# Selective scan on one core: the projection of u for both halves of the tokens side by side in two column tiles of TensorE

## Chip, cores, metric

One core of a Trainium2 chip runs the whole program: a two-layer network in one launch, all in float32. The metric is the time of one execution on the device, in microseconds (us). Engines are named as the profile names them: PE is TensorE (its weight loads are listed apart as PEld), DVE is VectorE, ACT is ScalarE, POOL is GpSimd, SP is SyncE, which issues the DMAs.

## The reference

Layer 0 is an attention over 4096 tokens of 4 images and a recurrent network over the same tokens; layer 1 is a selective scan and a mixture of experts. The change concerns the selective scan alone. With D = 256 channels, N = 16 states, R = 8 ranks, K = 4 directions and L = 4096 tokens of each of 4 images, it computes:

```
x_dbl = einsum('bkdl,kcd->bkcl', xs, x_proj_w)       # xs: u in 4 directions, c = R + 2N rows
dts_r, Bs, Cs = x_dbl[:, :, :R], x_dbl[:, :, R:R+N], x_dbl[:, :, R+N:]
dt = softplus(einsum('bkrl,kdr->bkdl', dts_r, dt_proj_w) + dt_proj_b)
h  = h * exp(dt * A) + (dt * u) * B                  # over the tokens, for each of D x N states
y  = sum over n of h * C
```

followed by sums over the directions, a norm, a gate and an output projection.

## The kernel before

`model` runs the stages one after the other: `attention`, `rnn`, `selective_scan`, `experts`. Inside the selective scan the function `scans` does the recurrence. A *window* is W = 500 tokens, that is NB = 4 blocks of T = 125, of one direction k; there are 33 windows in each of 4 directions, in the order k = 2, 3, 0, 1, so 132 windows. In k = 2 and 3 the tokens run backwards. A window has 16 *tiles*: 4 blocks times 4 quarters of the 16 states. A tile holds 4 states of all 256 channels (two halves h of 128 partitions) for 125 tokens, and one instruction of DVE, `tensor_tensor_scan` (L1315), runs its recurrence over 1016 columns.

Per tile: PE fills one of the two buffers `db` in PSUM with dt * u * B, by 16 small matmuls on 32 rows each (`fill`, L1291: for h = 0 on the rows of the block's number, for h = 1 two row groups further), and in the meantime adds zeros to the sum `y` (L1300). ACT computes the decays exp(dt * A) (L1256) into a ring ahead of time. DVE scans. ACT carries the last state of a block over to the next block's tile (`carry`, L1336). POOL multiplies the states by C (`times_c`, L1349), for which a DMA spreads the C rows over all partitions (`load`, L1268). Every second tile, PE sums the products over the states into `y` (`sum_of`, L1366: 8 matmuls in four 64x64 tiles). At a window's end ACT copies `y` out (`finish`, L1387); in all directions but k = 3 something that was there before is added to `y` first (`add_other`, L1377).

What the tiles of a window need is made ahead by the generator `project` (L1134 to L1241). It begins 40 turns before the window's first tile, is cut into steps by `yield turn`, and a loop over turns p runs each step when its turn comes. The order of all work is written out by hand: in each turn `finished`, `fill` of the next tile, `carry`, `scan`, `sums`, `times_c`, the load of C five turns ahead, `before`, `decay`, and then the steps of `project` that are due, first those of the window that began earlier. The steps, with their turns before the change:

- at -40 u is loaded; at -33 and -31 two matmuls (L1144) project its two halves of channels onto 128 rows x 500 tokens in `mm[:, 0]`: the dt ranks at rows 0 to 7 and again at 96 to 103, B at 32 to 47, C at 64 to 79;
- at -30 ACT adds a one and writes this to `xd` (L1149), and a DMA writes the C rows to `c_rows` in DRAM (L1151); at -29 ACT copies the B rows, in four overlapping quarters of a block, to `b_rows` (L1158);
- at -23 two matmuls of 9 rows (L1163) give dt for the two halves of channels in the two banks of `mm`, from rows 0 and 96 (so in two row tiles);
- at -22 to -20 ACT computes the softplus (L1182, L1185, L1187, L1188, L1190); at -19 and -18 DVE takes a maximum of two forms of it (L1195); at -17 POOL multiplies by u (L1198);
- at -15 the B rows are transposed (L1203) into `mm[:, 1]`; at -14 and -13 ACT copies them and dt * u (L1206, L1227), and DVE and POOL spread B onto diagonals (L1213, L1221);
- at -12 two DMAs write `b_other` (L1232), at -11 PE transposes dt * u (L1239), at -10 ACT copies it (L1241).

Since windows are 16 tiles apart, the step at -31 of one window falls in the turn of the step at -15 of the window before, and -33 in that of -17. The two PSUM banks `mm` are one tile that all these steps share, of which there is one.

```
        for h, turn in enumerate((-33, -31)):
            yield turn
            nc.tensor.matmul(
                x_ps[:, :W], w_x[:, h, k, :], v.u[:, h, :], start=h == 0, stop=h == ND - 1
            )
```

In the trace a float32 matmul has two records, one for each of its passes. The tiles of the first window take the turns 0, 2, 4, 5, 6 and so on; from then on each turn has one scan.

## Time and profile before

| what | value |
|---|---|
| time, median of 3 runs | 9429.01 us (9418.11 to 9439.51) |
| the profiled execution: its time | 9417.97 us |
| its span, first to last instruction | 9416.2 us |
| mean granted TensorE clock | 0.971 |
| first scan begins, last scan ends | 3582.7 us, 8748.5 us |
| scans (L1315) | 2112 of 2256 ns, 4671.3 us busy |
| products with C (L1349) | 2112 of 2152 ns, 4459.8 us busy |
| decays (L1256) | 4224 of 715 ns, 3018.2 us busy |
| projection of u (L1144) | 528 records, median 687 ns |
| dt (L1163) | 528 records, median 580 ns |
| xd (L1149), b_rows (L1158) | 132 each; 677 ns, 630 ns |
| softplus: L1182, L1185, L1187, L1188, L1190 | 132 each; 995, 991, 1133, 999, 1018 ns |
| dt maximum on DVE (L1195) | 264 of 654 ns |

The distance from one window's first scan to the next is 39.27 us in the directions 2, 0 and 1, and 38.43 us in direction 3; the first window takes 46.11 us. In the profile's groups, "idle before, releaser" tells how long an engine stood still just ahead of an instruction and what let it go on. Busy shares on the page are means over all stages; the fullest engine of the page need not be the one that sets the end of a stage.

### The profile page before, as it was taken

What the parts mean: (1) busy time and instruction counts of PE and PEld (TensorE: products, weight loads), DVE (VectorE), ACT (ScalarE), POOL (GpSimd) and SP (SyncE); (2) the same over time, 40 slices, a digit from 0 to 9 for tenths busy, and PEclk for the clock granted to TensorE, in tenths of its full rate; (3) what the DMA queues carried; (4) which work ended last, traced back from release to release, by engine and by line L of the source; (5) the groups of instructions that cost most, each with busy time, mean ns of one, the idle gap of its engine ahead of it and who ended that gap; (6) DMA issues with size and microseconds to landing.
All of it is one profiled execution on the core that took longest, in us unless ns stands there. A gap on an engine that the chain in (4) does not pass through costs nothing. (4 is left out here: it accounts for less than half of the span.)

```text
span 9416.2 us, 237919 instructions
## 1 busy us (share of the span) xinstructions
PE 8705.1 (92%) x102194; PEld 4318.3 (46%) x102194; DVE 8349.7 (89%) x5102; ACT 7121.8 (76%) x10926; POOL 4993.6 (53%) x2433
## 2 busy tenths in 40 slices
PE   7999999999988888999999999999999999999766
PEld 3333333333323334555555555555555555555223
DVE  6999999999978318999999999999999999999764
ACT  3888888888856467888888888888888888888321
POOL 0000000000001017999999999999999999999100
PEclk8999999999999898999999999999999999999887
DMA  4000000000011335666666656666666666666634
GB/s 169 36 8 35 8 10 35 8 8 8 10 52 56 115 135 151 173 173 173 172 171 167 165 164 162 161 171 173 173 173 173 173 173 173 173 173 168 231 111 184
DMA packets 530963, 1164.77 MB, mean 124 GB/s; under 512 B 76818, under 2 KB 444506, under 8 KB 502106
## 3 DMA queue, kind: packets, MB, share of 16 engines
q1 hardware_dynamic: 529882, 1149.30, 42.0%
q8 instruction: 807, 13.22, 0.6%
q14 instruction: 274, 2.24, 0.1%
HBM read 828.51 MB, written 182.15 MB: 107 GB/s over the span
## 5 line engine op out<-in xcount | busy, mean ns | idle before, releaser
L1315 DVE TENSOR_TENSOR_SCAN states<-decays,db 128x1016 f32<-128x1016 f32 x2112 | 4671.3, 2256 | 109.1 <-ACT decays L1336 60.5
L1349 POOL TENSOR_TENSOR products<-states,c_ring 128x1000 f32<-128x1000 f32 x2112 | 4459.8, 2152 | 294.8 <-DVE states L1315 173.4
L1256 ACT ACTIVATE decays<-dt,a_logs 128x500 f32<-128x500 f32 x4224 | 3018.2, 715 | 86.6 <-DVE states L1315 0.5
L1291 PEld LDWEIGHTS db<-b_diag,dtu_t 32*128 32x128 f32 x16896 | 2051.1, 187 | 1523.1 <-DVE states L1315 927.4
L1291 PE MATMUL db<-b_diag,dtu_t 32*128 32x128 f32 x16896 | 2429.4, 283 | 245.1 <-DVE states L1315 226.2
L1291 PE MATMUL db<-b_other,dtu_t 32*128 32x128 f32 x16896 | 2454.2, 284 | 0.0
L1300 PE MATMUL y<-zeros 32*128 32x128 f32 x14720 | 2122.0, 283 | 0.0
L1291 PEld LDWEIGHTS db<-b_other,dtu_t 32*128 32x128 f32 x16896 | 2048.0, 186 | 0.3 <-issue 0.2
L1366 PE MATMUL y<-products,ident 64*64 64x500 f32 x16896 | 2018.8, 592 | 1.1 <-POOL products L1349 1.1
L1300 PEld LDWEIGHTS y<-zeros 32*128 32x128 f32 x14720 | 1771.9, 186 | 0.0
L342 DVE TENSOR_TENSOR total<-total,ring 128x2048 f32<-128x2048 f32 x768 | 1706.9, 2285 | 32.3 <-ACT ring L304 31.6
masks.py:197 POOL MEMSET ident<- 128x128 f32 x6 | 1.2, 206 | 2915.6 <-SPq L181 2622.9
L304 ACT ACTIVATE ring<-sa 128x2048 f32<-128x2048 f32 (+3 forms) x667 | 1153.7, 1738 | 273.8 <-PE sa L289 262.2
L314 PE MATMUL av<-ring,v_at 128*32 128x256 f32 (+1 forms) x16128 | 1096.1, 389 | 6.2 <-ACT o L323 5.7
L1366 PEld LDWEIGHTS y<-products,ident 64*64 64x64 f32 x16896 | 541.2, 132 | 696.7 <-issue 568.1
L314 PEld LDWEIGHTS av<-ring,v_at 128*32 128x32 f32 x16128 | 421.4, 109 | 950.9 <-issue 748.9
L304 ACT ACTIVATE ring<-sb 128x1536 f32<-128x1536 f32 (+2 forms) x585 | 800.6, 1375 | 73.6 <-PE sb L289 63.8
L289 PE MATMUL sa<-q_at,k_at 32*128 32x512 f32 x4898 | 701.4, 640 | 20.6 <-issue 14.3
L289 PE MATMUL sb<-q_at,k_at 32*128 32x512 f32 x3294 | 624.0, 641 | 0.0
L1336 ACT COPY decays<-states 128x8 f32<-128x8 f32 x2048 | 405.3, 198 | 212.2 <-DVE states L1315 196.0
L289 PEld LDWEIGHTS sa<-q_at,k_at 32*128 32x128 f32 x4898 | 192.4, 183 | 354.6 <-issue 177.1
L339 DVE TENSOR_TENSOR total<-ring 128x2048 f32<-128x2048 f32 x128 | 288.6, 2287 | 67.0 <-ACT ring L304 66.6
(217 smaller groups left out, 8023.7 us busy)
## 6 DMA issues: line engine op xcount, KB each, us to landing
c_ring<-c_rows SPq DMA_DIRECT2D x2112, 250.0 KB, 4.8
b_other<-b_diag SPq DMA_DIRECT2D x264, 512.0 KB, 6.2
weights<-in_w SPq DMA_DIRECT2D x32, 1024.0 KB, 13.0
u<-u_r SPq DMA_DIRECT2D x60, 500.0 KB, 6.4
y_r<-sum SPq DMA_DIRECT2D x60, 500.0 KB, 4.7
u<-u_c SPq DMA_DIRECT2D x60, 500.0 KB, 6.4
y_c<-sum SPq DMA_DIRECT2D x60, 500.0 KB, 5.1
x<-x SPq DMA_DIRECT2D x96, 256.0 KB, 2.6
```

The costliest lines, as they stand in the source:

```text
L289: nc.tensor.matmul(s[:, m, :], k[rows, tokens(t)], q[rows, chunk(chunk_state["c"])], start=True, stop=True,)
L304: nc.scalar.activation(ring[:, lo : lo + n, :], s[:, at : at + n, :], AF.Exp)
L314: nc.tensor.matmul(chunk_state["av"][rows, some], chunk_state["v"][:, t, rows], ring[:, at + i, some], start=t == 0, stop=t == NJ - 1 and ...
L339: nc.vector.tensor_add(total, sums[g - 2], w)
L342: nc.vector.tensor_add(sums[g % 2], sums[g % 2], w)
L1256: nc.scalar.activation(to, dt, AF.Exp, scale=scale)
L1291: nc.tensor.matmul(bank.rearrange("p (n t) -> p n t", n=4)[:, :, to : to + 32], v.dtu[rows, h, s, :], b[rows, s, 4 * self.q : 4 * self.q + ...
L1300: nc.tensor.matmul(y[:, idle // 2, :P], zeros[rows], zeros[rows], start=False, stop=False)
L1315: nc.vector.tensor_tensor_scan(order(self.slot(states)), order(self.slot(decays, shift)), order(self.db[:, SKIP + shift :][:, : 2 * LANE]) ...
L1336: nc.scalar.copy(self.edge(later.slot(decays), later.v.into), last)
L1349: nc.gpsimd.tensor_mul(to, h, c)
L1366: nc.tensor.matmul(to, ident[rows, rows], of, start=begins, stop=ends)
```

## The change

The projection puts two halves of the window's tokens (blocks 0 and 1, blocks 2 and 3) beside each other: 64 rows each, in two column tiles of PE, where dt is at rows 0 to 7, B at 32 to 47 and C at 48 to 63 of each half. All four matmuls of 250 columns are issued at turn -33. `xd` has half as many columns and comes at -31, the B rows at -30, in two copies; the C rows go out in two DMAs. dt comes from rows 0 and 64, where the two halves of the tokens lie: four matmuls of 9 rows by 250 columns, bank j of `mm` for the half j of the tokens, and in each bank the two halves of the channels behind each other. So `mm` is read and written in another order afterwards, by a view of four runs of 250 columns; `e`, `bound` and `dt` keep their layout and are only viewed in the same way.

```diff
-DT_ROWS = 0, 96
+DT_ROWS = 0, 64
...
-    w_dt = cst.tile([P, K, P], F32, name="w_dt")
+    w_dt = cst.tile([P, K, ND, P], F32, name="w_dt")
...
-    for h, row in enumerate(DT_ROWS):
-        nc.sync.dma_start(w_dt[row : row + R + 1], a["w_dt"][:, :, h * P : (h + 1) * P])
+    for row in DT_ROWS:
+        nc.sync.dma_start(
+            w_dt[row : row + R + 1], a["w_dt"].rearrange("r k (h d) -> r k h d", h=ND)
+        )
...
+    def in_halves(of):
+        return of.rearrange("p h (j t) -> p h j t", j=2)
...
-        x_ps = mm[:, 0]
-        for h, turn in enumerate((-33, -31)):
-            yield turn
-            nc.tensor.matmul(
-                x_ps[:, :W], w_x[:, h, k, :], v.u[:, h, :], start=h == 0, stop=h == ND - 1
+        yield -33
+        x_ps = mm[:, 0, :WH]
+        for h in range(ND):
+            for j in range(2):
+                nc.tensor.matmul(
+                    x_ps[HALF * j : HALF * j + HALF],
+                    w_x[:, h, k, :],
+                    v.u[:, h, j * WH : (j + 1) * WH],
+                    start=h == 0,
+                    stop=h == ND - 1,
+                )
+        yield -31
+        xd = work.tile([P, WH], F32, tag="xd", name="xd", bufs=1)
+        nc.scalar.activation(xd, x_ps, AF.Identity, bias=one)
+        v.c_rows = dram.tile([NB, N, T], F32, tag="c", name="c_rows")
+        for j in range(2):
+            nc.sync.dma_start(
+                v.c_rows[2 * j : 2 * j + 2].rearrange("i n t -> n i t"),
+                xd[HALF * j + 48 : HALF * j + 48 + N].rearrange("n (i t) -> n i t", t=T),
             )
         yield -30
-        xd = work.tile([P, W], F32, tag="xd", name="xd", bufs=1)
-        nc.scalar.activation(xd, x_ps[:, :W], AF.Identity, bias=one)
-        v.c_rows = dram.tile([NB, N, T], F32, tag="c", name="c_rows")
-        nc.sync.dma_start(
-            v.c_rows.rearrange("i n t -> n i t"),
-            xd[64 : 64 + N].rearrange("n (i t) -> n i t", i=NB),
-        )
-        yield -29
         b_rows = work.tile([32 + N, NS, NB, 32], F32, tag="b_rows", name="b_rows", bufs=1)
-        for to, of in quartered(xd[32 : 32 + N], b_rows[32:], False):
-            nc.scalar.copy(to, of)
+        for j in range(2):
+            of = xd[HALF * j + 32 : HALF * j + 32 + N]
+            nc.scalar.copy(
+                b_rows[32:, :, 2 * j : 2 * j + 2],
+                bass.AP(of.tensor, of.offset, [of.ap[0], [STEP, NS], [T, 2], [1, 32]]),
+            )
         yield -23
-        pts = mm[:, :, :W]
-        for h, row in enumerate(DT_ROWS):
-            rows = slice(row, row + R + 1)
-            nc.tensor.matmul(pts[:, h], w_dt[rows, k, :], xd[rows], start=True, stop=True)
+        pts = mm[:, :, :W].rearrange("p j (h t) -> p h j t", h=ND)
+        for h in range(ND):
+            for j, row in enumerate(DT_ROWS):
+                rows = slice(row, row + R + 1)
+                nc.tensor.matmul(pts[:, h, j], w_dt[rows, k, h, :], xd[rows], start=True, stop=True)
...
-        bound = low[:, : ND * W].rearrange("p (h t) -> p h t", h=ND)
+        bound = in_halves(low[:, : ND * W].rearrange("p (h t) -> p h t", h=ND))
+        e = in_halves(e)
...
+        dt = in_halves(v.dt)
...
-            nc.vector.tensor_max(v.dt[:, h], pts[:, h], bound[:, h])
+            nc.vector.tensor_max(dt[:, h], pts[:, h], bound[:, h])
```

The weights are laid out to match: `w_x` has 64 rows a direction instead of 128, and each of the two row tiles holds the dt weights of all 256 channels.

More of the change, by code (lines that the diff above doesn't have):

```diff
@@ L1019, in scans @@
     TILES = Q * NB
-    HALF = P // 2
+    HALF, WH = P // 2, W // 2
     S = T + 2
@@ L1809, in apart @@
     def apart(w):
-        out = np.zeros((K, P, D), w.dtype)
-        out[:, 32 : 32 + N], out[:, 64 : 64 + N] = w[:, R : R + N], w[:, R + N :]
-        for row in DT_ROWS:
-            out[:, row : row + R] = w[:, :R]
+        out = np.zeros((K, P // 2, D), w.dtype)
+        out[:, :R] = w[:, :R]
+        out[:, 32 : 32 + N], out[:, 48 : 48 + N] = w[:, R : R + N], w[:, R + N :]
         return out
@@ L1840, in laid_out @@
         "b_conv": i["L1_conv_conv_b"].reshape(ND, P).T,
-        "w_x": apart(i["L1_conv_x_proj_w"]).reshape(K, P, ND, P).transpose(3, 2, 0, 1),
+        "w_x": apart(i["L1_conv_x_proj_w"]).reshape(K, P // 2, ND, P).transpose(3, 2, 0, 1),
         "w_dt": np.concatenate(
```

## The prediction

> **What bounds the kernel now.** I read the page first, then who waits on VectorE (DVE), then the timelines of one window of the scans (the one from 4375.07 to 4414.34 us), engine by engine. The page's first part names TensorE as the fullest engine:

> ```profile
> PE 8705.1 (92%) x102194; PEld 4318.3 (46%) x102194; DVE 8349.7 (89%) x5102; ACT 7121.8 (76%) x10926; POOL 4993.6 (53%) x2433
> ```

> That is an average over four layers. In the scans (first scan 3582.7, last 8748.5 us: 5165.8 us, 132 windows of 16 scans) all four engines are near full: in that one window of 39.27 us PE is busy 37.54, DVE 38.15, POOL 37.02 and ACT 33.16 us, at a granted clock of 1.00. So the question is which wait ends last. The waits of DVE over the stage:

> ```profile
> DVE states L1315 <- ACT decays L1336: 60.5, 99, 1.0
> DVE states L1315 <- PE db L1291: 28.5, 102, 2.2
> DVE dt L1195 <- ACT low L1190: 27.6, 125, 0.2
> ```

> All gaps of DVE in the stage add up to 137 us: no change of this stage that leaves DVE's own work alone can win more. The timeline of DVE in the chosen window shows where they sit:

> ```profile
> 4390.10 4.43 DVE L1315 TENSOR_TENSOR_SCAN states<-decays,db 128x1016 f32<-128x1016 f32 x2
> 4395.15 4.47 DVE L1315 TENSOR_TENSOR_SCAN states<-decays,db 128x1016 f32<-128x1016 f32 x2 [0.61 <-ACT decays L1336]
> 4399.79 4.43 DVE L1315 TENSOR_TENSOR_SCAN states<-decays,db 128x1016 f32<-128x1016 f32 x2 [0.17 <-PE db L1291]
> 4404.44 0.68 DVE L1195 TENSOR_TENSOR dt<-mm,low 128x500 f32<-128x500 f32 x1 [0.22 <-ACT low L1190]
> ```

> Numbering a window's scans 0 to 15, these waits stand before scans 8 and 10 and before the first dt maximum; 0.11 us stands before scan 6. The ACT timeline (idle time and its releaser in brackets):

> ```profile
> 4393.96 0.99 ACT L1387 COPY sum<-y 128x1000 f32<-128x1000 f32 x1 [1.62 <-PE y L1366]
> ...
> 4403.39 1.02 ACT L1190 ACTIVATE low<-low 128x1000 f32<-128x1000 f32 x1
> ...
> 4415.48 0.17 ACT L1206 COPY b_sb<-mm 128x16 f32<-128x16 f32 x1 [0.73 <-PE mm L1144]
> 4415.54 0.63 ACT L1227 COPY quarters<-dtu 128x512 f32<-128x512 f32 x1
> 4417.88 0.68 ACT L1149 ACTIVATE xd<-mm,one 128x500 f32<-128x500 f32 x1 [1.70 <-DVE b_diag L1213]
> ```

> From 4393.96 to 4404.41 ACT never stops, and the dt maximum starts when it gets through. It starts when PE's sums (L1366) end at 4393.90. The PE timeline, of the fills only the records after an idle stretch:

> ```profile
> 4380.81 0.37 PE L1291 MATMUL db<-b_diag,dtu_t 32*128 32x128 f32 x1 [0.60 <-DVE states L1315]
> ...
> 4408.45 1.11 PE L1144 MATMUL mm<-u,w_x 128*128 128x500 f32 x2
> 4410.10 0.37 PE L1291 MATMUL db<-b_diag,dtu_t 32*128 32x128 f32 x1 [0.54 <-DVE states L1315]
> ...
> 4414.33 1.10 PE L1144 MATMUL mm<-u,w_x 128*128 128x500 f32 x2
> ```

> From 4380.81 to 4393.90 PE has no gap either, and at 4380.81 it had waited for scan 1, which ended at 4380.75. So the window is one loop: PE from scan 1's end to the sums (13.09 us, with 0.06 before), ACT to the dt maximum (10.48), DVE without a gap from 4404.44 to the next window's scan 1 (4420.02, 15.58): 13.15 + 10.54 + 15.58 = 39.27 us, the measured period. Only what lies on this loop moves the time. In the 33 windows of k = 3 (38.43 us) nothing is added from another scan, PE's piece is about 0.84 us shorter, and the rest is the same.

> **The change, part by part.**

> *Projection of u, before.* Two matmuls of 500 columns, 1.11 us at 4408.45 (between the fills of scans 14 and 15) and 1.10 us at 4414.33 (between those of scans 0 and 1). Neither lies on the loop: behind the first PE idles 0.54 us, and behind the second it runs without a gap to about 4419.4 and idles 0.60 us before it may fill scan 3. The second is removed. That moves the fills of scans 1 and 2 about 1.0 us forward; scan 1 starts 1.2 us after its fill ends anyway, and the idle time before the fill of scan 3 grows from 0.60 to some 1.6 us. Value 0. What is late next is unchanged: that fill, which waits for scan 1.

> *Projection of u, after.* Four matmuls, 128 rows by 64 columns, 250 streamed columns each, all at the first place. Nearest row: four column tiles of full height in the attention,

> ```profile
> 2000.25 1.07 PE L314 MATMUL av<-ring,v_at 128*32 128x256 f32 x16
> ```

> Sixteen records of 256 columns in 1.07 us: the records start in fours, 7 ns apart, and the fours 0.216 to 0.24 us apart. So four steps (two passes of two accumulations), with side by side tiles for free. The new block also has four steps, of 250 columns: 1.05 us, against 1.11 now. The margin is 0.54 us: PE's next fill must start at 4410.10, and from there fill, sums and fill run without a gap to 4414.19, where the next scan 0 waits for nothing but has nothing to spare (it starts 0.15 us after the fill; before scan 6, which does wait, this distance is 0.14). So a block above about 1.7 us is paid in full in each window.

> [...] The row: in L314 the loads of the second pass (110 ns) start 2 ns after the first pass and the next pass follows at 0.216 us, on the same 128 rows. I take the row: 1.05 us, no cost.

> *dt from two row tiles.* Before, two matmuls of 9 rows by 500 columns on rows 0 and 96; after, four of 250 on rows 0 and 64. Per row tile two passes of 500 or four of 250: the same stream. What changes is who shares the row tiles with the fills on either side. In the windows that run backwards (k = 2, 3) these use rows 0 and 64, so dt starts after the fill and not beside it: up to 0.1 us later for the fill behind. Forwards (k = 0, 1) they use 32 and 96, so dt can lie beside them, up to 0.8 us of PE gained. Both act on the wait before scan 10 (0.17 us) and no further, because the dt maximum behind it waits for ACT in any case: what scan 10 gains or loses, up to 0.22 us, that wait gives back. Value 0.

> *ACT.* xd halves: 0.677 us for 500 columns becomes about 0.677 - 250 x 0.00084 = 0.47 (the slope from L1256 with 500 to L1187 with 1000 elements, and from 256 to 512 in the copies L1227, is 0.84 to 0.88 ns). b_rows becomes two copies of 256 elements, 0.41 each (row L1227) for 0.63. Sum 1.29 against 1.31 us. xd comes one turn sooner, ahead of the b_diag product on DVE, and no longer waits 1.70 us for it; b_sb loses its 0.73 us wait for L1144. All of it is ACT time between 4414.6 and 4420, and ACT idles 1.62 us later, at the sums, waiting for PE. What queues behind xd is the carry of scan 15, needed by scan 1 some 2.5 us later, and behind b_rows the carry of scan 0, ready about 4417.2 and needed at 4420.5 by scan 2. Value 0.

> *ACT on the loop.* L1182, L1185 and L1188 now walk mm in four runs of 250 instead of two of 500, and these do lie on the loop. Bound from below 0. From above: the copies of 8 and 16 runs (0.411 and 0.635 us for 256 and 512 elements) leave 198 and 208 ns beside the elements, so at most 1.3 ns a run, under 10 ns for the three. The two dt maxima on DVE likewise: runs of 32 in L1213 cost as much per element (1.09 ns) as the runs of 500 in L1195. I take 0; at the upper end 132 x 0.01 = 1.3 us.

> *DMA.* c_rows goes out as two writes instead of one: 0.32 us more on SP, and it is moved past one c_ring load. Now SP stands at this write until 4418.58, waiting for xd, with two c_ring loads queued behind; with xd sooner these leave some 3 us sooner. POOL waits 22.3 us for c_ring in the whole stage and is not on the loop. Value 0. The weights of the projection are half as large, those of dt twice: loaded once, behind VectorE's initial memsets.

> *Start of the scans.* Before the first scan there is no cover, and matmuls take twice as long there. In the second window's projection PE runs from 3559.21 to 3563.71; b_sb, the quarters and everything to the first scan follow it. After: four steps of about 0.45 us and the 0.6 us of B transposes, ready about 3561.8. The first scan comes about 2 us sooner. This is the one gain that I count.

> *Sum.* 132 x 0 - 2 us: span 9416.2 becomes 9414, and 9418.0 for the profiled run becomes 9416. The profiled run lies 11.0 us below the median of the three runs (9429.0), so on the median's scale: 9427.

> **The rivals.** No change: the loop of PE, ACT and DVE stays as it is. For it: its pieces add up to the period. 9427, with the spread of the three runs (-10.9, +10.4) about 9412 to 9444. A measurement of this kernel tells 0.2% (19 us) from no change.

> Slower, by the column tiles: the block at 4408.45 takes more than 1.7 us, and the fills of scans 15 and 0 slip. [...] Against it: L314 and the free start of its loads. [...]

> Slower, by the access patterns: three activations and two maxima on the loop have more runs; from 0.14 us a window on it shows. The copies speak against it. At 0.2 us a window: 9453.

> Faster: PE's relief shortens the loop after all, because the wait before scan 10 goes (0.17 x 99 + 0.09 x 33 = 20 us) and ACT is ready sooner than I think. Against it: ACT has no gap from 4393.96 on. 9407.

> **How the numbers follow.** No change 0.77, column tiles 0.09, patterns 0.06, faster 0.08. The range takes in nearly all of the first case and the near ends of the others: 9405 to 9448. Faster by over 0.2%: 0.08; slower: 0.15; within: 0.77.

> **What would show it.** Right: window periods of 39.27 and 38.43 us as before; one block of projection of some 1.05 us with PE idle about 0.6 us behind it; over 1.4 us idle before the fill of scan 3; no wait of xd for b_diag; the waits before scan 8 and the dt maximum still there; the wait before scan 10 smaller in k = 0, 1 alone and that before the maximum larger by as much. Wrong: a wait before scan 0 (column tiles), longer L1182, L1185 or L1188 (patterns), or a shorter stretch of ACT between sums and maximum.

## The result, and the profile after

The changed kernel takes 9579.67 us (median of 4 runs, 9575.05 to 9583.58), the kernel before beside it 9432.17 us: a ratio of 1.0158 [1.014, 1.0176]. The forecast was 9427 us, no change. The profiled execution has a span of 9581.7 us instead of 9416.2, and a mean granted clock of 0.95 instead of 0.971. The page's first part and the clock's row, after:

```profile
PE 8697.4 (91%) x103250; PEld 4349.3 (45%) x103250; DVE 8340.0 (87%) x5102; ACT 7126.9 (74%) x11058; POOL 4999.6 (52%) x2433
...
PEclk8999999999999978999999999999999999999887
```

Nothing here stands out: each engine works as long as before, in a longer span. The loss is in the scans: first scan to last takes 5313.5 us instead of 5165.7, which is 147.8 of the 165.5 us (13 lie ahead of the first scan and vary by as much between runs, 5 behind the last). The sums by stretch for 3600 to 8700 us, first after, then before; the third number from the end is the clock:

```profile
3600.00:8700.00 5100.00, 4711.70 (x67088) 2816.52 (x67088) 4823.12 (x2539) 4211.49 (x8119) 4690.07 (x2282) 0.96 0.60 166
```

```profile
3600.00:8700.00 5100.00, 4863.22 (x68001) 2868.17 (x67996) 4970.52 (x2612) 4317.95 (x8206) 4816.49 (x2347) 1.00 0.63 170
```

The clock of 0.96 instead of 1.00 is the figure to follow. DVE's waits in the scans after:

```profile
DVE states L1333 <- ACT decays L1274: 100.5, 99, 2.3
DVE states L1333 <- ACT decays L1354: 61.0, 101, 1.0
DVE states L1333 <- PE db L1309: 51.3, 89, 3.1
DVE dt L1213 <- ACT low L1207: 41.7, 115, 0.5
DVE states L1333 <- PE y L1318: 34.2, 55, 0.6
```

The second and the fourth of these were there before. The first and the last are new: 99 waits of 1 us, nearly all before scan 4, and 55 of 0.6 us before scan 6. (In 43 more windows the wait before scan 6 is put down to the fill, L1309, and is in the third line.) In DVE's timeline of one window (its first scan starts at 4416.54 us) they are the waits at 4428.03 and 4433.08:

```profile
4418.73 1.20 DVE L1231 TENSOR_TENSOR b_diag<-mm,ident 128x1024 f32<-128x1024 f32 x1
...
4422.60 4.42 DVE L1333 TENSOR_TENSOR_SCAN states<-decays,db 128x1016 f32<-128x1016 f32 x2
4428.03 4.43 DVE L1333 TENSOR_TENSOR_SCAN states<-decays,db 128x1016 f32<-128x1016 f32 x2 [1.01 <-ACT decays L1274]
4433.08 4.43 DVE L1333 TENSOR_TENSOR_SCAN states<-decays,db 128x1016 f32<-128x1016 f32 x2 [0.62 <-PE db L1309]
4438.13 4.47 DVE L1333 TENSOR_TENSOR_SCAN states<-decays,db 128x1016 f32<-128x1016 f32 x2 [0.62 <-ACT decays L1354]
```

The wait at 4428.03 is put down to ACT, but the fill of that scan (L1309) ends on PE at 4427.89: PE was late. PE's timeline of the same window, the projection, the sums and the pause:

```profile
4410.65 1.06 PE L1150 MATMUL mm<-u,w_x 128*64 128x250 f32 x8
...
4417.72 1.91 PE L1384 MATMUL y<-products,ident 64*64 64x500 f32 x16
4422.16 0.37 PE L1309 MATMUL db<-b_diag,dtu_t 32*128 32x128 f32 x1 [1.43 <-DVE states L1333]
4423.25 3.17 PE L1384 MATMUL y<-products,ident 64*64 64x500 f32 x16
```

The same 16 records take 1.91 us, and behind the pause of 1.43 us 3.17. The clock's record has one half-speed stretch here, from 4423.76 to 4427.17 us. Cutting the window at its edges:

```profile
4420.35:4423.76 3.41, 1.98 (x44) 1.40 (x42) 3.41 (x3) 1.56 (x4) 3.41 (x3) 1.00 0.63 156
4423.76:4427.17 3.41, 3.41 (x28) 1.27 (x23) 3.26 (x2) 2.90 (x6) 3.41 (x3) 0.50 0.13 16
4427.17:4430.59 3.41, 3.41 (x58) 2.71 (x59) 2.56 (x2) 2.76 (x7) 3.41 (x3) 1.00 1.00 223
```

A stretch of 3.41 us in which PE is busy for 1.98 us, then one at 0.50, then full speed again. In the scans 100 windows are *hit*: they have such a half-speed stretch behind the pause, some 6 to 7.5 us after their first scan. Before, apart from the start of the scans, there were only 2 half-speed stretches, at the first window of direction 0 and near the end; most kernels here have these too. The counts of hits below leave out that window and the last three (98 hits remain here); the expectations count all stretches (102 here, 85 in e1b_fill1). Each of the 100 lasts 3.413 us and begins on one fixed grid of 3413.33 ns (within 9 ns over the stage), so whether a window is hit depends on how the pause lies to the grid. One such piece of 3413.33 ns is called a grid window below.

The sum closes. A hit window takes 40.79 us in directions 2, 0 and 1 and 39.60 in direction 3, a window without a hit 39.15 and 38.31 (before: 39.27 and 38.43). Window by window against before: 87 hit ones of the first kind are longer by 134.5 us together, 13 of the second by 15.0, 30 without a hit are shorter by 3.5, and the first window is 1.4 us longer: 147.4 of 147.8 us. (The last window, 0.4 us longer, is the rest.)

### The profile page after: what moved, and what is told of

It reads as the page before. It is cut to its first block, busy times and chain, and to the rows that moved or that the text cites. A ratio compares the mean times of both kernels' runs of the same rounds, so it can differ in the third digit from the quotient of the medians.

```text
span 9581.7 us, 240293 instructions
## 1 busy us (share of the span) xinstructions
PE 8697.4 (91%) x103250; PEld 4349.3 (45%) x103250; DVE 8340.0 (87%) x5102; ACT 7126.9 (74%) x11058; POOL 4999.6 (52%) x2433
## 5 line engine op out<-in xcount | busy, mean ns | idle before, releaser
L1309 PE MATMUL db<-b_diag,dtu_t 32*128 32x128 f32 x16896 | 2447.1, 285 | 411.9 <-DVE states L1333 398.0
L1309 PEld LDWEIGHTS db<-b_diag,dtu_t 32*128 32x128 f32 x16896 | 2064.5, 188 | 1568.0 <-DVE states L1333 1094.3
L1309 PE MATMUL db<-b_other,dtu_t 32*128 32x128 f32 x16896 | 2445.8, 285 | 0.0
L1384 PE MATMUL y<-products,ident 64*64 64x500 f32 x16896 | 2157.3, 627 | 1.1 <-POOL products L1367 1.1
L1318 PE MATMUL y<-zeros 32*128 32x128 f32 x14720 | 2147.2, 285 | 0.0
L1309 PEld LDWEIGHTS db<-b_other,dtu_t 32*128 32x128 f32 x16896 | 2063.5, 188 | 2.2
L1318 PEld LDWEIGHTS y<-zeros 32*128 32x128 f32 x14720 | 1794.9, 188 | 0.0
L314 PE MATMUL av<-ring,v_at 128*32 128x256 f32 (+1 forms) x16128 | 1096.3, 389 | 6.2 <-ACT o L323 5.7
L1384 PEld LDWEIGHTS y<-products,ident 64*64 64x64 f32 x16896 | 566.6, 138 | 756.4 <-issue 633.4
L314 PEld LDWEIGHTS av<-ring,v_at 128*32 128x32 f32 x16128 | 421.5, 109 | 950.8 <-issue 748.9
```

The costliest lines, as they stand in the source:

```text
L314: nc.tensor.matmul(chunk_state["av"][rows, some], chunk_state["v"][:, t, rows], ring[:, at + i, some], start=t == 0, stop=t == NJ - 1 and ...
L1309: nc.tensor.matmul(bank.rearrange("p (n t) -> p n t", n=4)[:, :, to : to + 32], v.dtu[rows, h, s, :], b[rows, s, 4 * self.q : 4 * self.q + ...
L1318: nc.tensor.matmul(y[:, idle // 2, :P], zeros[rows], zeros[rows], start=False, stop=False)
L1384: nc.tensor.matmul(to, ident[rows, rows], of, start=begins, stop=ends)
```

## The experiments

Theory 1 says that the pause of PE before the fill of scan 3, grown from 0.60 to 1.43 us, halves the clock of the next 3.41 us. The rivals are named in the expectations. All edits are to the changed kernel unless the text says "before". Zero matmuls add zeros to `y` and are put at the end of the step at -13; they run in the pause.

### The pause filled (e1_fill5)

```diff
+        for _ in range(5):
+            if summed[-1] is not None:
+                nc.tensor.matmul(
+                    summed[-1][:, 0, :P], zeros[32:64], zeros[32:64], start=False, stop=False
+                )
         yield -12
```

> The changed kernel, with five matmuls of zeros (rows 32 to 63, 128 columns, 0.22 us each, added to y) at the end of turn -13 of the projection, that is in PE's idle time before the fill of scan 3. Theory 1 (the idle hole of 1.43 us halves PE's clock for 3.4 us in 102 of 132 windows): hole 0.3 us, no drop of the clock, window periods 39.15 and 38.31 us as in the undisturbed windows, time about 9432 - 132 x 0.12 = 9416. Theory 2 (the new tiles, columns of 64 and dt rows 0 and 64, are what costs): unchanged, about 9580, or slower. Theory 3 (PE's clock follows its mean load over a whole window): five times 0.22 us is what was removed, so also about 9430.

Measured: 9413.81 us against 9430.2, ratio 0.9983 [0.9977, 0.999]. No hits, periods 39.16 and 38.31. The zero matmuls (L1248), the pause of 0.33 us behind them and the sums at full speed, then the clock for 3600 to 8700 us:

```profile
4384.72 1.27 PE L1248 MATMUL y<-zeros 32*128 32x128 f32 x10
4386.32 0.37 PE L1314 MATMUL db<-b_diag,dtu_t 32*128 32x128 f32 x1 [0.33 <-DVE states L1338]
4387.42 1.91 PE L1389 MATMUL y<-products,ident 64*64 64x500 f32 x16
```

```profile
3600.00:8700.00 5100.00, 4838.74 (x70436) 2999.34 (x70436) 4959.77 (x2617) 4310.03 (x8351) 4825.18 (x2351) 1.00 0.62 171
```

PE has more work than after the change, and the loss is gone. What remains of the change is 0.12 us a window to the good. Theory 2 (the new tiles cost the time) is out, theory 3 (the mean load of PE) is not yet: the five put back about as much work as was removed.

### The pause without the change (e2_before_hole)

The kernel before, without its second projection matmul. It leaves out the contribution of half of the channels to dt, B and C.

```diff
-        for h, turn in enumerate((-33, -31)):
-            yield turn
-            nc.tensor.matmul(
-                x_ps[:, :W], w_x[:, h, k, :], v.u[:, h, :], start=h == 0, stop=h == ND - 1
-            )
+        yield -33
+        nc.tensor.matmul(x_ps[:, :W], w_x[:, 0, k, :], v.u[:, 0, :], start=True, stop=True)
```

> The kernel before, with the second matmul of the projection (turn -31) left out: dt, B and C then come from half of the channels. Nothing else is changed, full-height tiles of 128 columns, dt on rows 0 and 96. Theory 1: the same hole of 1.4 us opens, the clock drops in most windows, time 9560 to 9600. Theory 2: as before or a little faster, 9420 to 9432. Theory 3: as theory 1 or less, since all other work stands.

Measured: 9573.69 us, ratio 1.0155 [1.0139, 1.017], 97 hits. The pause and the sums behind it in one window:

```profile
4415.99 0.37 PE L1288 MATMUL db<-b_diag,dtu_t 32*128 32x128 f32 x1 [1.43 <-DVE states L1312]
4417.12 3.52 PE L1363 MATMUL y<-products,ident 64*64 64x500 f32 x16
```

No column tile, no new access pattern, and the whole loss: it comes from taking work out at turn -31, not from anything that the change puts in.

### Half of the projection back at -31 (e3_split)

```diff
-        yield -33
         x_ps = mm[:, 0, :WH]
-        for h in range(ND):
+        for h, turn in enumerate((-33, -31)):
+            yield turn
```

> The changed kernel, with the second pair of column-tile matmuls moved back to turn -31 (0.53 us there, xd and all else as in the changed kernel). Theory 1: hole about 0.9 us, most idle time in 3.41 us about 1.2 us, no drop, periods 39.15 and 38.31, time about 9416. Theory 2: tiles unchanged, 9580. Theory 3: total PE work unchanged, 9580.

Measured: 9433.69 us, 1.0001 [0.9994, 1.0007]; some 9416 were expected. The pause is 0.95 us, and the old place is hit once. Theory 3 is out: PE's work is that of the changed kernel, and nearly all of the loss is gone. But nine windows of directions 0 and 1 are hit at another place, some 35 us in, behind the projection block that is now half as long. There, grid windows with 1.49 to 1.80 us of idle time come before the half clock, but others with 1.53 to 1.73 us do not. (The ends of matmuls are modelled: in L1150 a record of 374 ns is followed by the next on its tile after 211. In these sums of idle time, here and below, the last 0.17 us of each record is not counted as busy.) Idle time alone does not decide.

### How much of the pause must be filled (e1b_fill1, e1c_fill3)

As e1_fill5, with one and with three zero matmuls.

> The same with one matmul of zeros instead of five: 0.22 us. Theory 1, with the limit read from the trace of the changed kernel (the clock dropped after stretches of 3.41 us with 1.49 to 1.70 us idle, and mostly not below 1.6): the most idle time in 3.41 us falls from 1.70 to about 1.48 us, so no drop or very few, time 9416 to 9440. Theory 2: 9580. Theory 3: a fifth of the removed work is back, so a fifth of the loss at most: about 9550.

Measured: 9546.82 us, 1.0127 [1.0111, 1.0142]; pause 1.22 us, 81 hits. Theory 1 with the limit that I had read into it missed: 1.50 us of idle time in 3.41 were still followed by a half clock. The time is the one that theory 3 gave, but e3_split had ruled that theory out, and so does the next run.

> The changed kernel with three zero matmuls (0.66 us of work) where five gave the time back and one did not. The hole of PE before the fill of scan 3 shrinks from 1.43 to some 0.8 us. Theory 1 (an idle share of PE in a window of 3.41 us, with a limit somewhere between the 1.06 us that never halved the clock and the 1.50 us that still did with one matmul): idle of about 0.9 to 1.1 us, below the limit, so no half clock: 9414, periods 39.16 and 38.31 us. Rival (what counts is each matmul's own cover of the hole, so that the loss falls in proportion to the work put in): about 9480. Between five and one this reads the limit.

Measured: 9430.52 us, 1.0 [0.9991, 1.0008]; pause 0.77 us, 8 hits. Neither 9414 nor 9480: three matmuls do nearly, but not quite, what five do, and the loss is not in proportion to the fill (81, 8 and no hits with one, three and five).

### Useful work in the pause (e4_other_in_hole, e6_other_and_fill), and without the change (e5_before_other)

```diff
-            w, turn = divmod(p - 23, TILES)
+            w, turn = divmod(p - 19, TILES)
             if turn == 0 and w in range(len(todo)):
                 add_other(todo[w])
```

e6 also has the five zero matmuls, in the windows of direction 3 alone; e5 is this edit in the kernel before.

> The changed kernel with the sums of the other scan (add_other, 8 records, some 1.07 us of PE) four turns earlier, where PE stands in the hole, and so out of the piece of PE that ends with the sums of the window. Theory 1 (the loop of PE, ACT and DVE sets the period, and the hole halves the clock): in the 99 windows of k = 2, 0, 1 the hole is filled with useful work, no half clock there, and the loop is shorter by most of 1.0 us: period about 38.2 to 38.4 instead of 39.27; in k = 3 nothing is added, so the hole and its half clock stay: 39.6. Sum 9430 - 95 + 33 x 1.2 x 0.75 = about 9355 to 9370. Rival (the sums of the other scan are not on the loop, some other wait of the same size takes their place): periods 39.1 in k = 2, 0, 1, about 9440.

> As the changed kernel with the sums of the other scan four turns earlier, and five zero matmuls in the hole in the windows where nothing is added from another scan (k = 3). Theory 1: no half clock anywhere in the stage, periods about 38.3 in all directions; 9430 - 132 x 0.12 - 99 x 0.85 = about 9330. Rival (the half clock in k = 3 has another cause than the hole): k = 3 stays at 39.6, about 9360.

> The kernel before with the sums of the other scan four turns earlier, and nothing of the change. The second projection matmul is still there, PE has only 0.60 us free before the fill of scan 3. Theory 1: the piece of PE from that fill to the sums gets shorter by 1.07 us at its end and starts some 0.5 us later, because the work is 0.47 us more than there is room: period 38.7 instead of 39.27 in 99 windows, about 9375. Rival (the same work merely moved along a PE that is full from scan 1 to the sums anyway): no change, 9430. The difference from the same move with the change in place (some 0.45 us a window) is what removing the second projection matmul is worth, once its room is used.

Measured: e4 9345.81 us, 0.9911 [0.9895, 0.9926]; e6 9335.01, 0.9895 [0.988, 0.991]; e5 9366.7, 0.9929 [0.9915, 0.9942]. In e4 the period is 38.31 us in directions 2, 0 and 1, and direction 3 is still hit (11 windows of 39.6). In e6 it is 38.31 in all directions: this version beats both kernels. DVE's timeline in e6, from scan 6 of one window into the next:

```profile
4379.65 13.29 DVE L1338 TENSOR_TENSOR_SCAN states<-decays,db 128x1016 f32<-128x1016 f32 x6
4393.16 0.68 DVE L1213 TENSOR_TENSOR dt<-mm,low 128x500 f32<-128x500 f32 x1 [0.22 <-ACT low L1207]
4393.75 2.26 DVE L1338 TENSOR_TENSOR_SCAN states<-decays,db 128x1016 f32<-128x1016 f32 x1
...
4406.36 2.26 DVE L1338 TENSOR_TENSOR_SCAN states<-decays,db 128x1016 f32<-128x1016 f32 x1
4408.53 0.67 DVE L1231 TENSOR_TENSOR b_diag<-mm,ident 128x512 f32<-128x512 f32 x1
4409.11 11.13 DVE L1338 TENSOR_TENSOR_SCAN states<-decays,db 128x1016 f32<-128x1016 f32 x5
```

The wait before scan 8 is gone (scans 6 to 11 are the first row); 0.22 us is left before the dt maximum, and 0.1 us each before scans 6 and 10: DVE's own work has become the bound. So the loop of the prediction was the right one.

In e5 the period is 38.43 us where I had expected 38.7. So the room that the change makes is worth 0.12 us a window, and not the 0.45 of the expectation. But 13 windows of e5 are hit some 21 us in, where PE never idles. Cut at the grid:

```profile
3964.91:3968.32 3.41, 3.41 (x44) 2.37 (x44) 3.41 (x2) 3.17 (x7) 3.30 (x3) 1.00 1.01 289
3968.32:3971.73 3.41, 3.41 (x22) 1.03 (x17) 2.83 (x2) 3.41 (x8) 3.41 (x3) 0.50 1.03 227
```

And what PE did in the first of the two, the fills left out:

```profile
3965.73 0.68 PE L1163 MATMUL mm<-xd,w_dt 9*128 9x500 f32 x1
3965.95 1.00 PE L1163 MATMUL mm<-xd,w_dt 9*128 9x500 f32 x3
```

PE busy for 3.41 of 3.41 us, and the next 3.41 us are at half clock. (Without the last 0.17 us of each record PE idles 0.27 us in this stretch, as against some 1.06 us in the emptiest 3.41 us of a window of the kernel before, which is not hit.) For 1.22 of these microseconds it works on 9 rows of 128. This broke the theory of idle time, and gave another: each record counts its streamed time (moving elements x 0.844 ns, from 0.216 us for 256 elements in L314) times the rows that it uses out of 128 times its columns out of 128; a grid window whose sum is below a limit is followed by one at half clock. This sum is called array time here. Over the ten traces up to here the best limit, 1.30 us of 3.41, is wrong for 21 of 14355 grid windows (332 were followed by a half clock); with idle time it is wrong for well over 100. The windows that it gets wrong lie within 0.1 us of the limit. A fit after the fact, so three more runs.

### Rows, columns or time (e8_one_full, e9_five_small, e10_five_nine_rows)

Theory 1a is idle time, 1b is array time with rows and columns, 1c is with rows alone. As e1_fill5, with other zero matmuls: one on all rows and columns; five of 32 rows by 32 columns; five of 9 rows by 128 columns.

```diff
+                nc.tensor.matmul(summed[-1][:, 0, :P], zeros, zeros, start=False, stop=False)
...
+                nc.tensor.matmul(summed[-1][:32, 0, :P], zeros[32:64, :32], zeros[32:64], start=False, stop=False)
...
+                nc.tensor.matmul(summed[-1][:, 0, :P], zeros[32:41], zeros[32:41], start=False, stop=False)
```

> The changed kernel with one zero matmul of 128 rows by 128 columns in the hole, where one of 32 rows by 128 columns left 85 half clocks and 9546.8. It takes PE as long (0.22 us), so PE stands still as long as there (about 1.2 us in the hole). Theory 1a (what counts is PE's idle time in a fixed window of 3.41 us): the same as with the small one, about 9545. Theory 1b (what counts is the work of the array: streamed time x rows/128 x columns/128; from the traces so far a window below about 1.30 us of 3.41 is followed by a half clock): the full matmul is worth four small ones (0.216 us of work), windows below the limit become few: 2 to 10 half clocks, about 9415.

Measured: 9418.76 us, 0.9989 [0.9983, 0.9996], no window hit at the pause.

```profile
4386.66 0.49 PE L1248 MATMUL y<-zeros 128*128 128x128 f32 x2
4388.16 0.37 PE L1312 MATMUL db<-b_diag,dtu_t 32*128 32x128 f32 x1 [1.01 <-DVE states L1336]
```

PE still idles 1.01 us there, more than the 0.77 with three small matmuls that left 8 hits. So rows count, and not time alone; theory 1a is out. (The matmul is not quite as short as I said: it ends 0.49 us after its start, the small one 0.38.)

> The changed kernel with five zero matmuls as in the run that gave the time back, but of 32 rows by 32 columns instead of 32 by 128. PE is as busy as there, the hole is as full (idle about 0.3 us), only the array has a quarter of the work (0.07 us instead of 0.27). Theory 1a (idle time): no half clock, 9414. Theory 1b (array work below 1.30 us in 3.41): still 45 to 80 half clocks of 1.3 to 1.6 us, 9480 to 9540.

Measured: 9415.48 us, 0.9988 [0.9981, 0.9995], no window hit at the pause (one is hit elsewhere, 26 us in). Theory 1b fell: with a quarter of the columns the five count in full. What stays is 1c: rows count, columns do not. The column weight had only looked right because all other narrow tiles of this stage lie side by side in pairs (64 columns each), and a pair then counts once by either rule.

> The changed kernel with five zero matmuls in the hole as in the run that gave the time back, but of 9 rows by 128 columns instead of 32 by 128: PE is as busy as there (the hole is filled to about 0.3 us), only fewer rows of the array work. Idle time (theory 1a): no half clock, 9414. Array work by rows alone (theory 1c, after the run with 32 columns: streamed time x rows/128, column tiles side by side counted once, limit about 1.30 us in 3.41): the five count 0.08 us instead of 0.27, so 35 to 75 windows fall below the limit: at 1.3 to 1.6 us each, 9465 to 9530.

Measured: 9507.26 us, 1.008 [1.0063, 1.0097]; 53 hits at the pause. PE's timeline in one window, the same in e9 above and in e10 below it:

```profile
4373.63 1.27 PE L1248 MATMUL y<-zeros 32*32 32x128 f32 x10
4375.13 0.37 PE L1312 MATMUL db<-b_diag,dtu_t 32*128 32x128 f32 x1 [0.23 <-DVE states L1336]
```

```profile
3720.48 1.27 PE L1248 MATMUL y<-zeros 9*128 9x128 f32 x10
3722.08 0.37 PE L1312 MATMUL db<-b_diag,dtu_t 32*128 32x128 f32 x1 [0.33 <-DVE states L1336]
3723.77 2.94 PE L1387 MATMUL y<-products,ident 64*64 64x500 f32 x16
```

Ten records, 1.27 us, a pause of 0.2 to 0.3 us: PE's time is the same. With 32 rows by 32 columns the clock stays, with 9 rows by 128 columns it is halved and the sums behind take 2.94 us instead of 1.91. Cut at the grid, e10:

```profile
3719.07:3722.49 3.41, 3.08 (x51) 2.49 (x46) 3.41 (x3) 0.95 (x4) 3.41 (x2) 1.00 0.62 167
3722.49:3725.90 3.41, 3.41 (x33) 1.85 (x33) 3.41 (x3) 2.87 (x6) 3.41 (x3) 0.50 0.24 63
```

With rows alone (the array time without its factor for columns, called row time from here on), 1.30 us in 3.41 is wrong for 35 of 18702 grid windows of all thirteen traces (389 half clocks). By this measure the lowest 3.41 us around the pause hold 1.72 us before and 1.10 after, 1.15 with one small zero matmul, some 1.25 with three, 1.32 with one on all rows, 1.37 with five of 32 rows, 1.18 with five of 9 rows (worked out: 1.37 - 10 x 0.108 x 23/128). Those far below 1.30 lose, the one just below it has 8 hits, the others have none. One thing these runs do not separate: each matmul also loads weights on as many rows as it uses (the page lists 103250 matmul records after the change and as many loads), so whether the streaming or the loads count isn't shown.

## Why the prediction was wrong

**The step that failed** is this: "the idle time before the fill of scan 3 grows from 0.60 to some 1.6 us. Value 0." The pause did grow, to 1.43 us, and by itself it cost nothing: with it filled by zeros the window is no shorter or longer than with the pause and no hit (39.16 and 39.15 us). But I had priced idle time of an engine as free, and had not asked what keeps PE's clock up: the prediction read a granted clock of 1.00 and took it as given. The removed matmul was 1.1 us of work on all 128 rows; without it the fills of scans 1 and 2 came earlier, and the 3.41 us around the pause fell from 1.72 to 1.10 us of row time, under the limit of 1.30. The half clock then makes the sums longer (3.17 us for 1.91) and the fill behind them, and those are on PE's piece of the loop: the window grows by 1.64 us (40.79 for 39.15), in direction 3 by 1.29. In 100 windows this cost 149.5 us, where the prediction had put nothing.

Idle time alone did not decide: the runs show 98 hits behind a pause of 1.43 us, none behind one of 1.01 us (e8), 8 behind one of 0.77 us (e1c), and 13 with PE busy for 3.41 of 3.41 us (e5). Here a grid window with less than some 38% of row time (1.30 us) was enough, and no window without work was needed.

**Right.** The loop of PE, ACT and DVE: taking 1 us out of PE's piece (e4, e6) shortens the period from 39.15 to 38.31 us, until DVE alone is the bound. The projection block: 1.06 us measured for 1.05. The loads of 64 columns lie beside the streams: in the block at 4410.65 us those of the later passes (137 ns) start 2 ns after a pass, and the next pass follows 0.211 us after that one. No wait came up before scan 0. xd 0.45 us for 0.47, and it no longer waits for b_diag; b_rows 0.41 twice. L1199, L1202 and L1205 take 995, 991 and 999 ns as before: the patterns cost nothing. The waits before scan 8 and the dt maximum stayed. The wait before scan 10 went in directions 0 and 1 alone, and there the wait before the dt maximum grew from 0.22 to 0.50 us: what one gained the other gave back, as the prediction said.

**Off.** Undisturbed windows are 0.12 us shorter, where I said 0: the first b_diag product starts 2.19 us after scan 0 instead of 2.28 and takes 1.20 us instead of 1.23. The same 0.12 us is there in e3, which has half of the projection at -31, and in e2, which has the old access patterns and in which xd still waits for b_diag. So neither the patterns nor that wait brings it; what the three have in common is less projection at turn -31, and how that acts isn't settled. The 2 us at the start of the scans can't be seen: the first scan starts between 3578 and 3599 us over these runs, and the first window is 1.4 us longer than before (47.5 for 46.1). This is the clock again: the scans begin at half clock (0.50 in the clock's record), which ends 30.0 us after the first scan in the kernel before and 32.9 us after it in the changed one. In all thirteen kernels the first window less half of that time is 31.0 to 31.1 us. Why the half clock ends later isn't settled.

**The rivals.** The slower one, by the column tiles, had a chance of 0.09, my estimate; its block of more than 1.7 us was not shown (1.06 us after the change), and e2 has the loss (9573.69 us) without any column tile. The case that happened was not among them.

**What the change is worth.** 0.17% with zeros in the pause (e1_fill5). With useful work there, e6 against e5 on the same chip: 9335.0 against 9366.7 us, and their stages 5072.5 against 5107.6, of which 131 x 0.12 = 16 us are shorter windows, and most of the rest is e5's 13 hits of about 1.5 us.

## What to carry to other kernels

Before work is taken off TensorE, look at the granted clock in the rows around it and add up what is left in any 3.41 us: streamed time times rows used of 128, column tiles side by side once. Here the clock held above some 1.30 us (38%) and was halved for the next 3.41 us below it, with few exceptions close to the limit (35 of 18702 grid windows), and full busy time (3.41 of 3.41 us in e5) with 9-row matmuls was no protection. A pause that appears ahead of a piece on the critical loop is a place for useful work. Here that was worth more (0.71% in the kernel before, e5; 1.05% together with the change and zeros, e6) than the change itself (0.17%). Zeros on many rows were a cheap stopgap (9413.81 us in e1_fill5 and 9418.76 in e8, for 9579.67).
